# Issuing a second mixture's slots during RWKV, and half of its shared experts behind its blocks, in a macaron network on one core

## The chip, the cores and the metric

The kernel runs on one core of a Trainium2 chip. It is one launch, and what counts is the device time of that launch in microseconds (us). TensorE does matmuls and transposes, VectorE (DVE) and ScalarE (ACT) do elementwise work and read the matmuls' results from PSUM, GpSimd (POOL) issues the indirect DMAs that move rows to and from slots, and SyncE (SP) issues the plain DMAs.

## The reference, cut to what matters

2048 tokens (two sequences of 1024) with 256 features pass through six residual steps, all in float32:

```python
x = L0_attn_x
x = x + 0.5 * L0_ffn(layernorm(x))     # 8 experts, 2 a token, hidden 176, shared hidden 352
x = x + L0_attn(layernorm(x))          # RWKV: time-mix, then channel-mix
x = x + 0.5 * L0_ffn(layernorm(x))     # the same mixture again
x = x + 0.5 * L1_ffn(layernorm(x))     # 32 experts, 6 a token, hidden 96, shared hidden 192
x = x + L1_attn(layernorm(x))          # linear attention
x = x + 0.5 * L1_ffn(layernorm(x))
```

A mixture is a routed part and a shared part, both of the normalized rows:

```python
topk_w, topk_idx = top_k(softmax(x @ gate_w), K)
g = silu(x @ w_gate[e]) * (x @ w_up[e])
routed = sum over chosen e of comb[t, e] * (g @ w_down[e])
shared = silu(x @ sw_gate) * (x @ sw_up) @ sw_down
```

RWKV here has no recurrence over time beyond a shift by one token: `h * mk + shift(h) * (1 - mk)` feeds keys, values and receptances, then the channel-mix does the same with a hidden width of 1024.

## The kernel before

The tokens lie in 16 tiles of 128 rows, `x[0]` to `x[15]`, in SBUF for the whole run. Four tiles (512 tokens) are a *quad*; there are four quads. The tile framework plans the order of the instructions on each engine with a simulated time line: what is written earlier has priority, but an instruction whose inputs are ready in the simulation can be put ahead of one written earlier. Within an engine the planned order is kept on the chip.

**A mixture** (`sparse_moe`) has these parts. `prep(b)` normalizes a quad (L124 to L157), transposes it into `xT` (L163, L420), multiplies it with the router (L424) and chooses the experts (`route`, L181 to L220). `plan(g)` counts rows per expert and gives each (token, expert) pair a slot in an array in DRAM, `xs` (L440 to L528); a quad's plan needs the counts of the quads before it. `scatter(g)` sends the normalized rows to their slots, one indirect DMA for each tile and choice: 8 a quad for L0, 24 for L1 (L538). `owners()` says which expert each block of 128 slots belongs to, once all quads are planned (L562 to L592). `weights(h)` picks the mixing weights (L601 to L608). `shared(t0, t1)` is the shared experts of some tiles (L631, L647, L654, L672; the result is added to `x` at L679). `blocks()` runs the experts' blocks one behind the other, 39 for L0: load the rows (L689), transpose (L698, L702), gate and up (L720), SiLU and product (L621, L622), transpose (L647), down (L737), store to `ys` (L746). `combine(g)` gathers a quad's results as soon as the blocks that can hold its rows are done (L757) and adds them to `x` (L769).

A block's load waits for every slot of its mixture (a dependence added by hand in `fetch`). While blocks are written, `Clock` runs other generators beside them: its own count of time decides between which blocks a quad's gathers or the next mixture's preparation are written, and `issue_after` keeps some of that behind the block just written.

**RWKV** is a list of jobs: time-mix of quad 0, time-mix of 1, channel-mix of 0, time-mix of 2, channel-mix of 1, and so on. `run` writes each job's `main` and, after its second step, the next job's `prep` (norms, transposes and shift). A time-mix's `prep` normalizes `x` into `xl` and that again into `n`. A channel-mix's `prep` also adds `xl` to `x` on GpSimd (L972), and its `main` adds `csr` there (L994), which completes the quad's `x`. All of RWKV's buffers are in one pool that is opened after the first mixture's pool is closed.

The order of the stages is: first L0 mixture (`begin`: prep, plan and scatter of all quads, then owners; shared experts of all 16 tiles; blocks, with gathers beside them), RWKV, second L0 mixture (`begin`, shared experts of all tiles, blocks), then the L1 mixture for two halves of the tokens (A and B), attention, and L1 again. Beside the second L0 blocks, `between` and `first_pass` gather the quads, prepare L1's half A and send its rows (48 indirect DMAs). When the L0 blocks are done, L0's weights are released and L1's down weights take their place.

Of the kernel before, what the change touches and what calls it, by code (L numbers as in the profile page):

```python
# [55 lines left out]
def macaron_kernel(ctx: ExitStack, tc: tile.TileContext, a: dict, out: bass.AP):  # L56
# [23 lines left out]

    numbers_i = const.tile([P, NT], I32, name="numbers_i")
    nc.gpsimd.iota(numbers_i, pattern=[[1, NT]], base=0, channel_multiplier=0)
    numbers = const.tile([P, NT], F32, name="numbers")
    nc.vector.tensor_copy(numbers, numbers_i)
    steps128 = const.tile([P, NT], F32, name="steps128")
    nc.vector.tensor_scalar(steps128, numbers, float(P), None, ALU.mult)

# [16 lines left out]
    nc.vector.tensor_scalar(others128, own128, -1.0, float(P), ALU.mult, ALU.add)  # L104

    row_of_i = const.tile([P, P], I32, name="row_of_i")
    nc.gpsimd.iota(row_of_i, pattern=[[1, P]], base=0, channel_multiplier=0)
    row_of = const.tile([P, P], F32, name="row_of")
    nc.vector.tensor_copy(row_of, row_of_i)
    row128 = const.tile([P, P], F32, name="row128")  # L110
    nc.vector.tensor_scalar(row128, row_of, float(P), None, ALU.mult)

# [267 lines left out]

    def sparse_moe(layer, w, name, x, xs, ys, moe, given=None, out=None):

# [8 lines left out]
        first = [moe_blocks(w, BT * (g + 1)) for g in range(NB)]  # L391
        taken = moe.tile([P, NT, E], F32, tag="taken", name=f"taken_{name}", bufs=2)
        comb = moe.tile([P, NT, E], F32, tag="comb", name=f"comb_{name}", bufs=2)
        slot = moe.tile([P, NT, E], F32, tag="slot", name=f"slot_{name}", bufs=2)
        top = back.tile([P, NT, 8], F32, tag="top", name=f"top_{name}", bufs=2)
        idx = back.tile([P, NT, K], I32, tag="idx", name=f"idx_{name}", bufs=3)
        wk = back.tile([P, NT, K], F32, tag="wk", name=f"wk_{name}", bufs=2)
        who = moe.tile([1, P], I32, tag="who", name=f"who_{name}", bufs=2)
        used = moe.tile([1, 1], I32, tag="used", name=f"used_{name}", bufs=2)
        xn, xT = {}, {}  # L400
        if given is not None:
            xn[0], xT[0] = given
        scattered, stored, groups = [], [], []

        def places(t):

            h, i = divmod(t, HT)
            if h not in xn:
                xn[h] = moe.tile([P, HT, D], F32, tag="xn", name=f"xn_{name}_{h}", bufs=2)
                xT[h] = moe.tile([P, DC, SEQ], F32, tag="xT", name=f"xTs_{name}_{h}", bufs=2)  # L410
            return xn[h], xT[h], i

        def prep(b):
            sub = f"{name}_{b}"
            ts = slice(BT * b, BT * b + BT)
            xb, xbT, o = places(BT * b)
            xb = [xb[:, o + i, :] for i in range(BT)]
            normalize(x[ts], xb, BT, sub)
            for c in range(DC):
                nc.scalar.copy(xbT[:, c, o * P : o * P + TB], transposed(xb, c, sub))  # L420
            lg = bank("pt", f"lg_{sub}")[:, 0 : BT * E].rearrange("p (t e) -> p t e", e=E)
            for i in range(BT):
                for c in range(DC):
                    nc.tensor.matmul(  # L424
                        lg[:, i, :],
                        xbT[:, c, (o + i) * P : (o + i + 1) * P],
                        w["router"][:, c, :],
                        start=(c == 0),
                        stop=(c == DC - 1),
                    )  # L430
            route(w, lg, sub, taken[:, ts, :], comb[:, ts, :])
# [99 lines left out]
        def scatter(g, rank=0):  # L531

            for t in range(BT * g, BT * g + BT):
                xb, _, i = places(t)
                for k in range(K):
                    yield from clock.call(rank)
                    with in_turn():
                        d = nc.gpsimd.indirect_dma_start(  # L538
                            out=xs,
                            out_offset=bass.IndirectOffsetOnAxis(  # L540
                                ap=idx[:, t, k : k + 1], axis=0
                            ),
                            in_=xb[:, i, :],
                            in_offset=None,
                        )
                    clock.called(d)
                    tc.declare_no_dep(
                        d.ins, group=f"slots_{name}", reason="a slot is one pair's"
                    )
                    tc.add_to_no_dep_group(f"slots_{name}", d.ins)  # L550
                    scattered.append(d.ins)
# [135 lines left out]
        def fetch(b):  # L687
            xb = moe.tile([P, D], F32, tag="xb", name=f"xb_{name}_{b}", bufs=XB)
            d = nc.sync.dma_start(out=xb, in_=xs[b * P : (b + 1) * P, :])  # L689
            for s in scattered:  # L690
                tc.add_manual_dep(d.ins, s.name, SYNC, reason="all tokens are at their slots")
            xbs[b] = xb

        def features(b):
            xb = xbs.pop(b)
            px = bank("pb", f"px_{name}_{b}")
            for c in range(DC):
                nc.tensor.transpose(  # L698
                    px[:, c * P : (c + 1) * P], xb[:, c * P : (c + 1) * P], ident
                )  # L700
            xbT = moe.tile([P, DC, P], F32, tag="xbT", name=f"xbT_{name}_{b}", bufs=2)
            nc.scalar.copy(xbT.rearrange("p c t -> p (c t)"), px[:, 0 : DC * P])  # L702
            xbTs[b] = xbT
# [29 lines left out]
        def outward(b):  # L733
            hT, e = bhT.pop(b), ws.pop(b)
            py = bank("py", f"py_{name}_b{b}")[:, 0:D]
            for k in range(C):
# [6 lines left out]
                )  # L743
            yb = moe.tile([P, D], F32, tag="yb", name=f"yb_{name}_{b}", bufs=3)
            clock.did(vector=nc.vector.tensor_copy(yb, py), tensor=mm)
# [58 lines left out]
        def blocks():  # L804
# [21 lines left out]

        return dict(
            prep=prep,
            plan=plan,
# [27 lines left out]
    def shifted(src, g, bias, tag, b, before, name):  # L857


        n = quad(rw["pool"], "xn", f"n_{name}", bufs=1)  # L860
        normalize(src, n, BT, name)
        hT = rw["pool"].tile([P, DC, TB + 1], F32, tag=tag, name=f"hT_{name}", bufs=2)
        if before is None:
# [13 lines left out]
    def mixed(hT, v, tag, name):  # L877

        pool = rw["pool"]
        o = pool.tile([P, DC, TB], F32, tag=tag, name=f"{tag}_{name}", bufs=1)  # L880
        for c in range(DC):
            t = pool.tile([P, TB], F32, tag="mixt", name=f"mixt_{tag}_{name}_{c}", bufs=2)
            nc.scalar.activation(t, hT[:, c, 0:TB], AF.Copy, scale=rw[f"1-{v}"][:, c : c + 1])
# [30 lines left out]
    def time_mix_job(b):  # L914
# [3 lines left out]
        def prep():  # L918
            xl = quad(rw["pool"], "xl", f"xl_{name}", bufs=3)
            normalize(xb, xl, BT, f"{name}_a")  # L920
# [231 lines left out]

    def run(jobs):
        jobs[0][0]()
        for j, (_, main) in enumerate(jobs):
            nxt = jobs[j + 1][0] if j + 1 < len(jobs) else None
            for n, _ in enumerate(main()):
# [3 lines left out]
            if nxt is not None:  # L1161
                nxt()

    xs, ys = {}, {}
# [16 lines left out]

    rwkv = [time_mix_job(0)]
    for b in range(1, NB):
        rwkv += [time_mix_job(b), channel_mix_job(b - 1)]
    rwkv.append(channel_mix_job(NB - 1))
# [38 lines left out]

    with tc.tile_pool(name="rwkvw", bufs=1) as weights:
        with tc.tile_pool(name="moe_L0_0", bufs=1) as pool:
            m = sparse_moe("L0", w0, "L0_0", x, xs["L0"], ys["L0"], pool)
            begin(m)
            load_rwkv(weights)
            for h in range(2):  # L1230
                m["weights"](h)
            every_step(m["shared"](0, NT))
            added = set()
            clock.begin(0, given_rows(m, range(NB), added))
            all_of(m["blocks"]())
            settle(lambda: NB - 1 in added)
        for h in range(2):
# [5 lines left out]
            )  # L1243
        clock.block.clear()
        with tc.tile_pool(name="rwkv", bufs=1) as pool:
            rw["pool"] = pool
            run(rwkv)

# [4 lines left out]

    m0 = sparse_moe("L0", w0, "L0_1", x, xs["L0"], ys["L0"], moe_pool)
    begin(m0)
    for h in range(2):
        m0["weights"](h)
    every_step(m0["shared"](0, NT))

    m1, m2 = {}, {}  # L1260
    added0, summed, ready1, ready2 = set(), {0}, [set(), set()], [set(), set()]
    sent1, sent2 = [set(), set()], [set(), set()]
# [17 lines left out]
    def first_pass(h):  # L1280

        for g in range(2):
            yield from wait(lambda: 2 * h + g in added0)
            if g == 0:
                m1[h] = half(0, h)
            yield from onward(m1[h], g, ready1[h])
# [51 lines left out]
    for h in range(2):  # L1338
        clock.begin(1 + h, first_pass(h))
    all_of(m0["blocks"]())  # L1340
    settle(lambda: 1 in ready1[0])
    l0_stack.close()
# [87 lines left out]
```

## Time and profile before

| what | us |
|---|---|
| median of 3 runs | 1716.1 (1712.1 to 1722.52) |
| profiled execution, whole | 1729.15 |
| its span | 1727.4 |
| TensorE busy (share of the span) | 1334.3 (77%) |
| VectorE busy | 737.4 (43%) |
| ScalarE busy | 625.8 (36%) |
| GpSimd busy | 522.7 (30%) |

The span is the time between the first and the last instruction of the one execution that was profiled. Lines of the profile name a group of instructions by source line, engine, operation and tiles (`out<-in`, buffer numbers left out; `L` in a tile's name stands for L0 or for a numbered use). PEld is TensorE's loading of weights, which overlaps its matmuls. In brackets stands the idle time ahead of an instruction and what ended it; "issue" is a wait for nothing that the profile shows, "remote" a release whose author it cannot name. The granted clock is the share of full speed at which TensorE was allowed to run.

| stretch, us | what runs |
|---|---|
| 0 to 136 | first L0 mixture: routing, slots, shared experts |
| 136 to 241 | its 39 blocks |
| 241 to 257 | last gathers, first time-mix norms |
| 257 to 474 | RWKV |
| 474 to 594 | second L0 mixture: routing, slots, shared experts |
| 594 to 781 | its blocks; L1 half A prepared beside them |
| 781 to 1727 | L1 mixture, attention, L1 mixture |

### The profile page before, as it was taken

How to read it: one execution, taken by the hardware profiler on the slowest of the kernel's cores; microseconds unless marked ns; L12 is line 12 of the kernel's file. 1: busy time of each engine (PE TensorE's matmuls, PEld its weight loads, DVE VectorE, ACT ScalarE, POOL GpSimd, SP SyncE). 2: the span in 40 equal slices, each digit the busy share in tenths (PEclk: the TensorE clock that was granted, in tenths of full speed). 3: DMA queues.
4: the chain of work that ended last, by engine and by line, in shares of the span. 5: the costliest groups of instructions: out<-in, count | busy, mean ns of one | idle time of the engine just before them, and what ended most of it. 6: DMA issues, size and time to landing. Idle time of an engine off the chain costs nothing. (4 is left out here: it accounts for less than half of the span.)

```text
span 1727.4 us, 22283 instructions
## 1 busy us (share of the span) xinstructions
PE 1334.3 (77%) x6100; PEld 1009.8 (58%) x6100; DVE 737.4 (43%) x2510; ACT 625.8 (36%) x1670; POOL 522.7 (30%) x562
## 2 busy tenths in 40 slices
PE   6699967899978998627559768975669994668972
PEld 5577743566666776415449656764357772447951
DVE  4422458555243234215234437432347642425543
ACT  3123346876432333302215334432124442123520
POOL 2400330111133012663350333022744014546055
PEclk8599988899967998767579869886878985888986
DMA  9502439500082033227235545232344332336653
GB/s 297 161 28 86 143 106 330 204 1 0 1 209 70 24 117 99 100 95 207 91 127 181 169 146 156 76 107 78 122 138 147 98 97 87 120 98 207 199 158 97
DMA packets 195164, 214.89 MB, mean 124 GB/s; under 512 B 40892, under 2 KB 178012, under 8 KB 195036
## 3 DMA queue, kind: packets, MB, share of 16 engines
q1 hardware_dynamic: 170460, 146.22, 27.3%
q0 software_dynamic: 24576, 67.14, 12.3%
q8 instruction: 59, 0.97, 0.2%
q14 instruction: 69, 0.57, 0.1%
HBM read 103.04 MB, written 110.23 MB: 123 GB/s over the span
## 5 line engine op out<-in xcount | busy, mean ns | idle before, releaser
L757 POOL DMA_INDIRECT yk_L<-ys_L,idx_L x64 | 61.3, 958 | 288.2 <-DMA ys_L<-yb_L 251.7
L720 PE MATMUL pg_L_b<-L0gu,xbT_L 128*128 x312 | 108.5, 471 | 0.0
L737 PE MATMUL py_L_b<-L0down,hT_L_b 88*128 x312 | 87.4, 405 | 10.0 <-issue 6.4
L631 PE MATMUL pg_L<-L0sgu,xTs_L 128*128 128x352 f32 x256 | 89.2, 488 | 3.7 <-DVE h_L L622 3.7
L538 POOL DMA_INDIRECT xs_L<-xn_L,idx_L x64 | 61.9, 967 | 99.0 <-DVE idx_L L528 42.1
L538 POOL DMA_INDIRECT xs_A<-axl_at,idx_L_1A x48 | 47.2, 982 | 128.1 <-DVE idx_L_1A L528 114.1
L538 POOL DMA_INDIRECT xs_B<-axl_at,idx_L_1B x48 | 46.4, 966 | 129.0 <-DVE idx_L_1B L528 115.0
L757 POOL DMA_INDIRECT yk_L_0A<-ys_A,idx_L_0A x48 | 46.7, 973 | 120.8 <-DMA xb_L_0A<-xs_A 67.5
L737 PEld LDWEIGHTS py_L_b<-L0down,hT_L_b 88*128 88x128 f32 x312 | 62.3, 204 | 33.5 <-issue 9.8
L622 DVE TENSOR_TENSOR h_L_b<-g_L_b,pg_L_b 128x176 f32<-128x176 f32 x78 | 26.1, 336 | 120.1 <-ACT g_L_b L621 85.5
L757 POOL DMA_INDIRECT yk_L_1B<-ys_B,idx_L_1B x48 | 46.0, 958 | 72.6 <-DMA xb_L_1B<-xs_B 50.4
L631 PEld LDWEIGHTS pg_L<-L0sgu,xTs_L 128*128 128x128 f32 x256 | 49.4, 202 | 28.1 <-DVE h_L L622 5.3
L720 PEld LDWEIGHTS pg_L_b<-L0gu,xbT_L 128*128 128x128 f32 x312 | 55.3, 196 | 17.9 <-issue 1.0
L892 PE MATMUL pkk_cm<-mk_cm,w_WkeyT 128*128 128x512 f32 x128 | 62.0, 615 | 2.9 <-ACT sk_cm L984 2.9
L720 PE MATMUL pg_L_0B_b<-L1gu,xbT_L_0B 128*128 x272 | 63.3, 361 | 0.2
L720 PE MATMUL pg_L_1A_b<-L1gu,xbT_L_1A 128*128 x272 | 62.3, 356 | 1.4 <-issue 1.3
L720 PE MATMUL pg_L_0A_b<-L1gu,xbT_L_0A 128*128 x272 | 62.1, 354 | 1.0 <-issue 1.0
L538 POOL DMA_INDIRECT xs_B<-xn_L_0B,idx_L_0B x48 | 46.6, 970 | 52.9 <-DVE ends_L_0B L574 30.3
L737 PE MATMUL py_L_1A_b<-L1down,hT_L_1A_b 96*128 x136 | 48.1, 445 | 17.0 <-issue 13.1
L720 PE MATMUL pg_L_1B_b<-L1gu,xbT_L_1B 128*128 x272 | 60.3, 347 | 0.0
L757 POOL DMA_INDIRECT yk_L_0B<-ys_B,idx_L_0B x48 | 46.4, 966 | 45.6 <-DVE x L769 29.4
L757 POOL DMA_INDIRECT yk_L_1A<-ys_A,idx_L_1A x48 | 46.9, 977 | 43.3 <-DVE x L769 26.9
(641 smaller groups left out, 3381.5 us busy)
## 6 DMA issues: line engine op xcount, KB each, us to landing
xs_A<-zero SPq DMA_DIRECT2D x1, 10112.0 KB
xs_B<-zero SPq DMA_DIRECT2D x1, 10112.0 KB
xb_L<-xs_L SPq DMA_DIRECT2D x78, 128.0 KB
ys_L<-yb_L SPq DMA_DIRECT2D x78, 128.0 KB
xb_L_0A<-xs_A SPq DMA_DIRECT2D x68, 128.0 KB
ys_A<-yb_L_0A SPq DMA_DIRECT2D x68, 128.0 KB
xb_L_0B<-xs_B SPq DMA_DIRECT2D x68, 128.0 KB
ys_B<-yb_L_0B SPq DMA_DIRECT2D x68, 128.0 KB
```

Of the source, the lines that this page charges most:

```text
L538: d = nc.gpsimd.indirect_dma_start(out=xs, out_offset=bass.IndirectOffsetOnAxis(ap=idx[:, t, k : k + 1], axis=0), in_=xb[:, i, :], in_offs ...
L622: nc.vector.tensor_tensor(dst, g, pg[:, width : 2 * width], ALU.mult)
L631: nc.tensor.matmul(pg, xbT[:, c, i * P : (i + 1) * P], w["sgu"][:, c, u, :, :].rearrange("p z w -> p (z w)"), start=(c == 0), stop=(c == D ...
L720: nc.tensor.matmul(pg, xbT[:, c, :], w["gu"][:, c, bass.ds(e, 1), :, :].rearrange("p e z h -> p (e z h)"), start=(c == 0), stop=(c == DC - 1),
L737: mm = nc.tensor.matmul(py, hT[0:HP, k, :], w["down"][:, bass.ds(e, 1), k, :].rearrange("p e d -> p (e d)"), start=(k == 0), stop=(k == C ...
L757: d = nc.gpsimd.indirect_dma_start(out=yk, out_offset=None, in_=ys[0 : n * P, :], in_offset=bass.IndirectOffsetOnAxis(ap=idx[:, t, k : k + ...
L892: nc.tensor.matmul(ps, w[:, c, oc * P : (oc + 1) * P], src[:, c, :], start=(c == 0), stop=(c == DC - 1),)
```

## The change

The second L0 mixture is made before RWKV is run, and the slots of quads 0, 1 and 2 are issued behind the channel-mix of that quad (`slots_of`, run from `behind`). Their normalized rows are in RWKV's one-buffer `xn` tile and their transposed rows in a one-buffer `xTe`; since neither outlives the quad, `again(b)` repeats norm and transposes for the shared experts later. Quad 3 is prepared behind RWKV as before, then come the owners.

Of both L0 mixtures' shared experts, tiles 0 to 7 are done ahead of the blocks and tiles 8 to 15 behind them. In the second mixture, `again(2)` comes behind the blocks too, and the preparation of L1's half B waits for `summed0`.

The first two time-mix `prep`s are run by the clock beside the first L0 blocks, each once its quad's results are added (`first_jobs`). The buffers that they use (`xn`, `xl`, `h1T`, `mk`, `mixt`) lie in a new pool, `rwkv_in`, that is opened ahead of the first mixture's pool. To make room, index tiles at the start are merged and some of the mixture's small tiles have one buffer.

```diff
-    def sparse_moe(layer, w, name, x, xs, ys, moe, given=None, out=None):
+    def sparse_moe(layer, w, name, x, xs, ys, moe, given=None, out=None, bufs=2, early=None):
...
+        def features_of(b, xb, xbT, o, sub):
+            normalize(x[BT * b : BT * b + BT], xb, BT, sub)
+            for c in range(DC):
+                nc.scalar.copy(xbT[:, c, o * P : o * P + TB], transposed(xb, c, sub))
+        def again(b):
+            xb, xbT, o = places(BT * b)
+            features_of(b, [xb[:, o + i, :] for i in range(BT)], xbT, o, f"{name}_{b}_again")
         def prep(b):
             sub = f"{name}_{b}"
             ts = slice(BT * b, BT * b + BT)
-            xb, xbT, o = places(BT * b)
-            xb = [xb[:, o + i, :] for i in range(BT)]
-            normalize(x[ts], xb, BT, sub)
-            for c in range(DC):
-                nc.scalar.copy(xbT[:, c, o * P : o * P + TB], transposed(xb, c, sub))
+            if early is not None and b < NB - 1:
+                xb, o = early(sub), 0
+                xbT = rw["pool"].tile([P, DC, TB], F32, tag="xTe", name=f"xTe_{sub}", bufs=1)
+            else:
+                xb, xbT, o = places(BT * b)
+                xb = [xb[:, o + i, :] for i in range(BT)]
+            sent[b] = xb
+            features_of(b, xb, xbT, o, sub)
...
     def shifted(src, g, bias, tag, b, before, name):
-        n = quad(rw["pool"], "xn", f"n_{name}", bufs=1)
+        n = quad(rw["in"], "xn", f"n_{name}", bufs=1)
...
-    def run(jobs):
-        jobs[0][0]()
+    def run(jobs, begun, behind):
         for j, (_, main) in enumerate(jobs):
-            nxt = jobs[j + 1][0] if j + 1 < len(jobs) else None
+            nxt = jobs[j + 1][0] if j + 1 < len(jobs) and j + 1 >= begun else None
             for n, _ in enumerate(main()):
                 if nxt is not None and n == 1:
                     nxt()
                     nxt = None
             if nxt is not None:
                 nxt()
+            if j in behind:
+                behind[j]()
...
+    def slots_of(b):
+        def slots():
+            m0["prep"](b)
+            m0["plan"](b)
+            every_step(m0["scatter"](b))
+        return slots
     for b in range(1, NB):
+        behind[len(rwkv) + 1] = slots_of(b - 1)
         rwkv += [time_mix_job(b), channel_mix_job(b - 1)]
...
-            every_step(m["shared"](0, NT))
+            every_step(m["shared"](0, HT))
             added = set()
+            def first_jobs():
+                for b in range(begun):
+                    yield from wait(lambda: b in added)
+                    rwkv[b][0]()
             clock.begin(0, given_rows(m, range(NB), added))
+            clock.begin(1, first_jobs())
             all_of(m["blocks"]())
+            all_of(m["shared"](HT, NT))
             settle(lambda: NB - 1 in added)
...
+        m0 = sparse_moe("L0", w0, "L0_1", x, xs["L0"], ys["L0"], early_pool, bufs=1,
+            early=lambda sub: quad(rw["in"], "xn", f"xn_{sub}", bufs=1))
+        run(rwkv, begun, behind)
...
-    m0 = sparse_moe("L0", w0, "L0_1", x, xs["L0"], ys["L0"], moe_pool)
-    begin(m0)
+    m0["home"]["pool"] = moe_pool
+    slots_of(NB - 1)()
+    m0["owners"]()
+    for b in range(2):
+        m0["again"](b)
+    every_step(m0["shared"](0, HT))
     for h in range(2):
         m0["weights"](h)
-    every_step(m0["shared"](0, NT))
...
     def first_pass(h):
         for g in range(2):
             yield from wait(lambda: 2 * h + g in added0)
             if g == 0:
+                yield from wait(lambda: h in summed0)
                 m1[h] = half(0, h)
...
     all_of(m0["blocks"]())
+    m0["again"](2)
+    all_of(m0["shared"](HT, NT))
+    summed0.add(1)
     settle(lambda: 1 in ready1[0])
     l0_stack.close()
```

## The prediction

> **What bounds the kernel now.** I read the page first, then the busy times of stretches cut at the stage borders, then TensorE's timeline around each border, then the waits inside the one stretch that looked wrong. The stage borders come from TensorE's own tiles: the first L0 mixture's blocks (`pg_L_b`) run from 136.3 to 240.8 us, RWKV's first projection (`pk_tm`) starts at 257.2, its last matmul ends at 473.4, the second L0 mixture's blocks start at 594.2, and the first L1 blocks (`pg_L_0A_b`) at 815.1.
>
> Busy times of stretches (columns: stretch, its length, then busy us and instructions of PE, PEld, DVE, ACT, POOL, then the granted TensorE clock, the DMA share and GB/s):
>
> ```profile
> 136.00:241.00 105.00, 100.37 (x473) 74.86 (x471) 40.57 (x114) 38.52 (x118) 22.93 (x24) 1.00 0.38 119
> 241.00:257.00 16.00, 1.94 (x8) 1.57 (x8) 11.78 (x48) 8.12 (x14) 7.66 (x8) 0.56 0.27 82
> 257.00:308.00 51.00, 40.11 (x97) 20.75 (x98) 42.37 (x79) 33.71 (x47) 5.23 (x8) 0.80 0.94 334
> 308.00:474.00 166.00, 160.61 (x568) 104.60 (x566) 76.89 (x175) 110.56 (x153) 19.16 (x26) 0.98 0.11 40
> 474.00:538.00 64.00, 48.20 (x252) 40.13 (x253) 26.31 (x177) 17.62 (x35) 23.87 (x25) 0.64 0.65 162
> 538.00:594.00 56.00, 56.00 (x237) 41.19 (x236) 16.35 (x53) 17.39 (x57) 7.72 (x8) 0.95 0.10 33
> 688.00:781.00 93.00, 45.88 (x193) 30.97 (x192) 25.29 (x103) 17.40 (x41) 53.91 (x56) 0.70 0.28 97
> ```
>
> TensorE is the bound in blocks, in the later part of RWKV (160.6 busy of 166) and in the shared experts. It is not the bound in three places, and there the change works: the 16 us after the first blocks (2 busy), the 64 us of the second mixture's routing (48 busy, at a granted clock of 0.64, so much less in work), and the 93 us from 688 on, where GpSimd is busiest.
>
> TensorE's timeline (start, us, engine, line, operation):
>
> ```profile
> 112.99 3.12 PE L631 MATMUL pg_L<-L0sgu,xTs_L 128*128 128x352 f32 x10
> 120.98 3.12 PE L631 MATMUL pg_L<-L0sgu,xTs_L 128*128 128x352 f32 x10
> ...
> 257.22 6.77 PE L892 MATMUL pk_tm<-mk_tm,w_WkT 128*128 128x512 f32 x8 [3.44 <-DVE mk_tm L884]
> 272.19 3.70 PE L892 MATMUL pk_tm<-mk_tm,w_WkT 128*128 128x512 f32 x8 [0.45 <-DVE mk_tm L884]
> ...
> 475.39 1.06 PE L163 MATMUL pt_L<-ident,xn_L 128*128 128x128 f32 x8 [1.99 <-DVE xn_L L154]
> 594.23 1.35 PE L720 MATMUL pg_L_b<-L0gu,xbT_L 128*128 x4
> ```
>
> The same place in the pattern of shared experts comes back after 8.0 us, which is two tiles: 4.0 us a tile. From the last RWKV matmul to the second blocks are 594.2 - 473.4 = 120.8 us. GpSimd's first slot of that mixture goes out only at 495.6:
>
> ```profile
> 495.56 1.02 POOL L538 DMA_INDIRECT xs_L<-xn_L,idx_L  x1 [20.77 <-ACT xTs_L L420]
> ```
>
> And in 688 to 781 the waits are not for data that take long to make:
>
> ```profile
> DVE h_L_b L622 <- remote: 23.7, 2, 19.6
> PE pg_L_0A L631 <- issue: 21.7, 1, 21.7
> ACT g_L_b L621 <- remote: 22.3, 1, 22.3
> ```
>
> While GpSimd sends trains of 24 slots (688 to 719, 738 to 768), what TensorE finished reaches ScalarE and VectorE 5 to 22 us late, and the mixture's last blocks crawl: block 33 starts at 716.4 where the even pace of 2.49 us would put it at 676.
>
> **The change, part by part** (times of the profiled execution: span 1727.4, whole 1729.15 us; the median of the runs shown is 1716.1, 0.8% lower, so a difference is carried over to it as it stands).
>
> *First mixture.* Eight tiles of shared experts leave the front: 8 x 4.0 = 32 us, and the blocks start at 104 in place of 136.3. Nothing else holds them there: the last slot goes out at 89.1 and the load of the first block's rows is issued at 91.6. The 32 us come back behind the blocks, where TensorE had the 16 us with 2 busy. So the time-mix could begin at 257.2 - 16 = 241, if the first two quads' norms cost nothing beside the blocks. They do cost: a norm of the L1 kind beside blocks held block 26 back by 13.3 - 2.5 = 11 us (656.2 to 669.5), a quad's gathering and adding by 1.8 us (196.3 after 192.3). Two quads: 4 to 22 us, taken at 8 because there is no routing in them. Net -8. The first eight projections also find a warm clock (6.77 against 3.70 us, -3) and the mix for the keys is made early (-1). Sum -12; bounds -25 (all hidden, and the vector work of 257 to 308 shortened too) and 0.
>
> *Slots in RWKV.* Norm, eight transposes, 16 router matmuls, counts and ranks, and eight slots for each of three quads now lie in a stretch where TensorE has 5 us of slack in 166. TensorE's own share is 5.6 us for the first quad at a warm clock (1.06 + 2.17 + 0.34 + 1.62 + 0.36) and about 6.2 for a later one (estimate: its rows at half clock, halved): 18 us for three. Above that lie the in-order hand-overs. Alone, one quad followed another every 14 us (counts at 501.9, 515.6, 529.6), 42 for three; an L1 quad's norm and plan beside blocks took 11 + 6.6 us, 52 for three. I take 28, nearer the low end: RWKV offers the planner other matmuls between the hand-overs, the blocks' pipeline did not. GpSimd's slots (8 x 1.27 = 10 us a quad) lie in a queue that is 19 of 166 us busy; behind a slot that waits for its indices stand the residual adds (L972, L994), and `csr`, which has two buffers, waits for those. The norms of time-mix and channel-mix now share one `xn` buffer with rows that the slots' DMAs still read. Both are hidden as long as the planner puts the next channel-mix's norm, whose inputs are ready a whole job earlier, ahead of the slots.
>
> ScalarE pays here too: each quad needs the square root and the exponential between SiLU and sigmoid, some four table loads. The row: a load took 1.28 us (at 478.85), and the activation behind it started 0.01 us after it ended, so 5 us a quad beside 110.6 busy of 166; that is inside the 28. The Trainium skill ("ScalarE: Activation LUTs", What ACT_TABLE_LOAD costs) adds a drain of about 1.38 us to each switch; by it three quads would cost an estimated 17 us more and the sum below would nearly vanish. The trace shows no such drain, so I leave it out.
>
> The skill speaks against the slots in another way ("SBUF — State Buffer", SBUF: two separate sides): GpSimd cannot write descriptors while VectorE runs certain copies, and an indirect DMA beside them may take about 3100 ns where 620 was normal. Here, with VectorE 41% busy (474 to 538), slots kept their 962 ns (median of 64, longest 1140), and RWKV's VectorE is 46% busy; no charge. By the page, 24 slots would hold `xn` an estimated 60 us longer in all.
>
> *Before the second blocks.* 120.8 us become what one quad needs: idx 21 us after RWKV's end as now (495.6), owners till about 27 (535.7 to 538.5 now, some 5 us behind the last count), and behind that what remains of eight shared tiles when four tiles' first products are done by then, as they were at 492: 4 x 2.4 + 8 x 1.6 = 23 us. That is 50; the last quad's slots end at 32 and are covered. The repeated norms and transposes of quads 0 and 1 (16 transposes, 2 us) hide in the 27 us. So -71 (bounds -78 and -60).
>
> *Behind the second blocks.* Quad 2's repeated transposes (3 us with copies) and eight shared tiles, 32 us: +35. TensorE had 47 us idle in 688 to 781, but that idle time is the late signals; its queue is in order, and the shared experts stand behind the blocks that wait. When the last train ended at 768, blocks and L1's own shared tiles were still to do, so I charge all 35; the other end is 0. Quad 2's added rows (L769) now also wait for its repeated norm, and group B's first norm for the shared half; group B's slots ended at 900 and its blocks began at 1002, so 35 us are covered.
>
> Removed index tiles at the start: five small instructions of 0.13 to 0.54 us ahead of data that arrive at 2.9 us; nothing. The zero fills (23 MB) start earlier and end long before the first slot in RWKV; nothing.
>
> Sum: -12 + 28 - 71 + 35 = **-20 us**: 1709 profiled, **1696** for the median.
>
> **The rivals.** *The tail is hidden:* the shared half runs in the 47 idle us. For it: that much is idle. Against: the order of the queue. Then -20 - 35 = -55: 1661.
>
> *Nothing left:* the slots cost as an L1 quad beside blocks, 17.4 us each, 52: -12 + 52 - 71 + 35 = +4, no change that can be measured.
>
> *Slower: the single `xn` buffer.* If buffers are handed out in the written order, the channel-mix norm waits until a quad's slots have left: 21 us chain + 10 us of slots, 31 a quad with nothing covering it, 93 for three: -12 + 93 - 71 + 35 = +45: 1761. With the time-mix of some 20 us between as cover it is less. It decides from (12 + 71 - 35) / 3 = 16 us a quad. For it: TensorE is full there and VectorE's and ScalarE's queues are in order. Against: the trace has the second quad's time-mix statistics (247.6) ahead of the first quad's mixes (256.4), so work moves ahead of its written place.
>
> **How the numbers follow.** 0.5% (8.6 us) is about what a measurement of this kernel can tell from no change. My forecast (9 to 45 us gained, 1671 to 1707) gets 0.47, the hidden tail 0.12, nothing left 0.15, slower 0.26. Faster is 0.59, same 0.15, slower 0.26. The terms' best ends give -25 + 18 - 78 + 0 = -85, their worst 0 + 52 - 60 + 35 = +27, and the buffer rival +45. Leaving out about a tenth on each side, I give 1645 to 1750.
>
> **What would show it.** Right: first blocks at about 104; `pk_tm` around 249; the last RWKV matmul at 473.4 - 12 + 28 = about 489; the second blocks 50 us after it, about 540; `pg_L_0A_b` about 20 us earlier than 815.1, with the L0 shared tiles between the last L0 block and L1's shared tiles. Wrong: idle stretches of TensorE over 10 us in RWKV ended by `xn` or by an indirect DMA (the buffer rival); L0's shared half finished before the second train ends (hidden tail); or late signals spreading into RWKV once slots go out there.

## The result, and the profile after

The changed kernel takes 1767.03 us (median of 4 runs, 1763.81 to 1769.4) where the kernel before takes 1717.87 us (4 runs): a ratio of 1.0287, 95% interval 1.0249 to 1.0324. The forecast was 1696; it went the other way, to where the rival of the single `xn` buffer (1761) had put it. The profiled execution has a span of 1766.4 us, 39 us over the one before. The medians differ by 49: the profiled execution before, of 1729.15 us, is longer than each of the 4 runs (1722.52 at most). What follows explains the 39.

The stage borders, from TensorE's tiles (us; the start of the matmul named):

| border | before | after | after - before | foreseen |
|---|---|---|---|---|
| first L0 blocks | 136.3 | 103.8 | -32.5 | 104 |
| first projection (`pk_tm`) | 257.2 | 255.5 | -1.7 | 249 |
| channel-mixes of quads 0 to 3 (`pkk_cm`) | 307.6, 357.6, 404.9, 441.9 | 302.5, 389.5, 478.2, 503.2 | -5, +32, +73, +61 | |
| last RWKV matmul | 473.0 | 548.5 | +75.5 | 489 |
| second L0 blocks | 594.2 | 612.3 | +18.1 | 540 |
| last of these | 736.1 | 759.3 | +23.2 | |
| first L1 blocks (`pg_L_0A_b`) | 815.1 | 885.2 | +70.1 | 795 |
| last of these | 984.9 | 1022.6 | +37.7 | |
| end | 1727.4 | 1766.4 | +39 | |

Busy times of stretches of the changed kernel, in the columns used before (stretch, its length, then PE, PEld, DVE, ACT, POOL, the granted TensorE clock, the DMA share, GB/s):

```profile
302.00:342.00 40.00, 39.51 (x140) 26.53 (x141) 16.87 (x41) 26.38 (x37) 5.45 (x8) 0.95 0.57 190
342.00:390.00 48.00, 30.80 (x95) 19.17 (x94) 27.15 (x89) 16.78 (x28) 11.76 (x13) 0.66 0.06 23
390.00:415.00 25.00, 25.00 (x82) 15.46 (x81) 4.24 (x8) 14.24 (x21) 0.10 (x1) 0.98 0.00 1
415.00:478.00 63.00, 39.91 (x138) 26.07 (x136) 30.87 (x104) 23.43 (x35) 14.08 (x16) 0.72 0.05 17
550.00:613.00 63.00, 49.88 (x227) 37.31 (x228) 23.85 (x112) 21.07 (x54) 10.77 (x12) 0.76 0.61 150
759.00:885.00 126.00, 79.23 (x347) 56.51 (x346) 45.80 (x178) 30.94 (x73) 53.25 (x55) 0.75 0.40 118
885.00:1022.00 137.00, 111.08 (x615) 97.09 (x615) 50.97 (x169) 52.03 (x202) 34.74 (x36) 0.84 0.49 151
```

RWKV, which had TensorE busy for 160.6 of 166 us, now has two holes: 342 to 390, where quad 0's slots are, and 415 to 478, where quad 1's are. In them TensorE is 64% and 63% busy, at a granted clock of 0.66 and 0.72; in the full stretch between them the clock is 0.98. No other engine is full in the holes either: behind TensorE, VectorE is the busiest, at 57% and 49%.

TensorE's timeline in the first hole (start, us, engine, line, operation, and in brackets the idle time ahead and what ended it):

```profile
342.09 3.60 PE L908 MATMUL pv_tm<-mv_tm,w_WvT 128*128 128x512 f32 x8
352.18 0.66 PE L156 MATMUL pt_L<-ident,xn_L 128*128 128x128 f32 x2 [6.49 <-DVE xn_L L147]
353.87 1.54 PE L156 MATMUL pt_L<-ident,xn_L 128*128 128x128 f32 x6 [1.02 <-ACT xn_L L143]
356.55 3.63 PE L436 MATMUL lg_L<-L0router,xTe_L 128*128 128x8 f32 x16 [1.14 <-ACT xTe_L L415]
363.17 0.34 PE L452 MATMUL count_L<-ones,taken_L 128*8 128x1 f32 x8 [2.99 <-DVE taken_L L202]
...
365.17 3.76 PE L908 MATMUL pr_tm<-mr_tm,w_WrT 128*128 128x512 f32 x4
...
376.63 4.67 PE L920 MATMUL po_tm<-w_WoT,rv_tm 128*128 128x256 f32 x12 [1.66 <-DVE rv_tm L968]
384.00 1.78 PE L156 MATMUL pt_cm<-ident,n_cm 128*128 128x128 f32 x8 [2.70 <-DVE n_cm L147]
```

The routing steps of quad 0 (`pt_L`, `lg_L`, `count_L`) stand ahead of the third time-mix's receptances (`pr_tm`) in TensorE's queue. Each step waits for VectorE or ScalarE, and what is ready behind it waits too: `mr_tm`, from which the receptances are made, is written by 332.2. And four `pr_tm` products then take 3.76 us; in RWKV's full stretches four such products take 1.88. Only at 384.0 come the transposes of the channel-mix's norm (`pt_cm`), and with them the 25 us of solid work that the hole had lacked. Their norm itself was held up, as all engines' timeline shows:

```profile
353.02 0.30 ACT L132 ACTIVATE rstd_cm<-mv_cm,eps 128x4 f32<-128x4 f32 x1
...
371.31 1.01 POOL L549 DMA_INDIRECT xs_L<-xn_L,idx_L  x1 [27.73 <-DVE idx_L L540]
...
380.72 0.96 POOL L549 DMA_INDIRECT xs_L<-xn_L,idx_L  x1 [0.31 <-issue]
...
383.22 1.09 ACT L143 ACTIVATE n_cm<-xl_tm,shift_cm,rstd_cm 128x256 f32<-128x256 f32 x2 [9.00 <-DMA xs_L<-xn_L,idx_L]
```

The channel-mix's statistics are there at 353.3. Its norm `n_cm` is written 30 us later, into the buffer from which quad 0's eight slots have just been read. The 9.00 us in the bracket are only what ScalarE had been idle; the wait of the data is the 30. In the second hole the statistics are there at 435.0, quad 1's slots leave from 460.4 to 470.2, and the norm starts at 471.7. There the wait stands alone in TensorE's timeline:

```profile
457.70 3.74 PE L920 MATMUL po_tm<-w_WoT,rv_tm 128*128 128x256 f32 x14 [0.23 <-DVE slot_L L529]
472.49 1.97 PE L156 MATMUL pt_cm<-ident,n_cm 128*128 128x128 f32 x8 [11.04 <-DVE n_cm L147]
```

Quad 2's slots open no hole. `behind` runs them after the last but one channel-mix, and the last one's norm is written ahead of them. From the channel-mix of quad 2 to RWKV's end are 70.3 us, and 68.0 in experiment 3, which has no slots in RWKV; the two spacings before that are 87.0 and 88.7 against 46.9 and 49.1.

### The profile page after: what moved, and what is told of

The parts are those of the page before. It is cut to its first block, busy times and chain, and to the rows that moved or that the text cites. A ratio compares the mean times of both kernels' runs of the same rounds, so it can differ in the third digit from the quotient of the medians.

```text
span 1766.4 us, 22400 instructions
## 1 busy us (share of the span) xinstructions
PE 1352.0 (77%) x6124; PEld 1016.8 (58%) x6124; DVE 743.3 (42%) x2543; ACT 625.5 (35%) x1683; POOL 523.3 (30%) x561
## 5 line engine op out<-in xcount | busy, mean ns | idle before, releaser
L731 PE MATMUL pg_L_b<-L0gu,xbT_L 128*128 x312 | 112.2, 484 | 0.2
L748 PEld LDWEIGHTS py_L_b<-L0down,hT_L_b 88*128 88x128 f32 x312 | 64.2, 211 | 32.0 <-issue 11.6
L665 ACT COPY hT_L_b<-ph_L_b 88x256 f32<-88x256 f32 x78 | 28.6, 368 | 88.9 <-PE ph_L_b L658 47.8
```

The source lines that it names most:

```text
L665: nc.scalar.copy(hT[0:m, lo:hi, :].rearrange("p k t -> p (k t)"), pt[0:m, lo * P : hi * P])
L731: nc.tensor.matmul(pg, xbT[:, c, :], w["gu"][:, c, bass.ds(e, 1), :, :].rearrange("p e z h -> p (e z h)"), start=(c == 0), stop=(c == DC - 1),
L748: mm = nc.tensor.matmul(py, hT[0:HP, k, :], w["down"][:, bass.ds(e, 1), k, :].rearrange("p e d -> p (e d)"), start=(k == 0), stop=(k == C ...
```

## The experiments

The runs were made on several chips: on that of experiments 1 to 4 the kernel before takes 1488, on the others 1717 to 1741. So times are compared as ratios to the kernel before on the same chip, and stages by their length; RWKV, from the start of its first projection to that of its last matmul, runs at one pace on all of them (211.8, 210.7, 210.7 and 210.9 us in the versions without slots: 3, 7, 10 and 12). It took 215.8 us before (215.0 in experiment 6) and 293.0 in the change (293.1 in 4 and 5).

**1. Slots' rows in a buffer of their own.**

```diff
-                e2 = pool.tile([P, TB], F32, tag="e2", name=f"e2_{name}_{oc}", bufs=1)
+                e2 = dp
...
-                av = pool.tile([P, TB], F32, tag="av", name=f"av_{name}_{oc}", bufs=1)
+                av = rv[:, oc, :]
...
-            early=lambda sub: quad(rw["in"], "xn", f"xn_{sub}", bufs=1),
+            early=lambda sub: quad(rw["in"], "xe", f"xe_{sub}", bufs=1),
```

> The early slots' rows get a buffer of their own; to make room, two scratch tiles of the time-mix are written in place of others. In the changed kernel the channel-mixes of quads 0, 1 and 2 start 87.0 and 88.7 us apart (50.0 and 47.3 before), and RWKV ends at 549. Buffer theory: the channel-mix norm waits until eight slots have been read out of xn, so with its own buffer the norm goes at about 354 in place of 383, the spacing falls to 60 to 65 us, RWKV ends at 495 to 505, and the time is 1710 to 1725. Hand-over theory (the router's chain in TensorE's in-order queue holds the time-mix's rest): spacing stays over 80 and the time within 1755 to 1770.

Measured: ratio 1.0145 (1.0103 to 1.0188), channel-mixes 77.3 and 67.9 us apart, RWKV 265.4 us. That lies between the two theories: the buffer is worth 28 us of RWKV, not 50. VectorE's and TensorE's timelines of this version say where the rest went (the norm, then its transposes):

```profile
354.51 0.64 DVE L147 TENSOR_SCALAR n_cm<-xl_tm,rstd_cm,shift_cm 128x256 f32<-128x256 f32 x2
```

```profile
347.87 1.94 PE L156 MATMUL pt_L<-ident,xe_L 128*128 128x128 f32 x8 [7.03 <-DVE xe_L L147]
352.65 3.64 PE L436 MATMUL lg_L<-L0router,xTe_L 128*128 128x8 f32 x16 [2.84 <-ACT xTe_L L415]
362.10 0.34 PE L452 MATMUL count_L<-ones,taken_L 128*8 128x1 f32 x8 [5.82 <-DVE taken_L L202]
...
368.74 1.11 PE L156 MATMUL pt_cm<-ident,n_cm 128*128 128x128 f32 x4
```

The norm is now done at 355.2, as the buffer theory said. But its transposes start at 368.7: they stand behind the routing steps in TensorE's queue, and TensorE waits 5.8 us for `taken_L` with them ready.

**2. Slots one job later** (those of quads 0 and 1; those of quad 2 stay where they are).

```diff
-        behind[len(rwkv) + 1] = slots_of(b - 1)
+        behind[min(len(rwkv) + 2, 2 * NB - 2)] = slots_of(b - 1)
```

> The slots of quads 0 and 1 are issued one job later, behind the next channel-mix's norm; the one xn buffer stays. Buffer theory: the channel-mix no longer waits for slots, the next time-mix's norm does, and that has a whole channel-mix of 25 us as cover: spacing of the channel-mixes 55 to 65 us, RWKV ends at 490 to 510, time 1710 to 1730. Hand-over theory: the same chain stands in the same queues one job later, spacing over 80, RWKV's end about 549, time 1755 to 1770.

Measured: ratio 0.9982 (0.9961 to 1.0003); channel-mixes 45.6 and 60.7 us apart, RWKV 239.0 us. The first spacing is under the pace before (50.0). Without slots RWKV takes 211 us, so slots cost 82 in the change and 28 here: with the one shared buffer, place alone is worth 54. TensorE's timeline after it shows the cover:

```profile
344.82 3.60 PE L908 MATMUL pkk_cm<-mk_cm,w_WkeyT 128*128 128x512 f32 x8
...
352.12 1.04 PE L156 MATMUL pt_L<-ident,xn_L 128*128 128x128 f32 x8
353.93 1.98 PE L908 MATMUL pkk_cm<-mk_cm,w_WkeyT 128*128 128x512 f32 x4 [0.77 <-ACT sk_cm L1000]
...
360.65 1.40 PE L436 MATMUL lg_L<-L0router,xTe_L 128*128 128x8 f32 x12
361.91 1.11 PE L920 MATMUL po_tm<-w_WoT,rv_tm 128*128 128x256 f32 x4
```

The same steps lie between products of the channel-mix, whose norm is now written ahead of them. From 345 to 390 no gap reaches 2 us, and the eight transposes take 1.04 us in place of 2.2.

**3. No slots in RWKV** (the line with `behind[...]` is taken out, the second mixture begins behind RWKV as before, so no norm is repeated; the first mixture's part of the change and both halved shared experts stay).

> All four quads' slots of the second mixture are issued behind RWKV, as before the change; the first norms beside the blocks and the halved shared experts stay. If the slots alone lengthen RWKV, it ends at 465 to 472 (473.4 before, 549 changed) and the second blocks start 85 to 92 us behind it, at about 555 to 562 (612 changed), so the time is 1712 to 1722. If the norms moved beside the blocks or the clock lengthen RWKV too, it ends above 490 and the time is over 1730.

Measured: ratio 0.9933 (0.9909 to 0.9958); RWKV 250.6 to 462.4, second blocks 87.1 us behind it. The slots alone lengthen RWKV: 293 - 211 = 82 us, and they take 87.1 - 63 = 24 off the stretch behind it. Without them the change is 0.7% faster than the kernel before. Busy times of RWKV in the change, in this version and in version 2:

```profile
255.50:548.90 293.40, 239.82 (x825) 153.57 (x823) 132.92 (x370) 141.93 (x207) 44.37 (x55) 0.85 0.26 86
250.60:462.80 212.20, 197.92 (x681) 125.34 (x679) 117.73 (x251) 142.54 (x199) 23.83 (x34) 0.97 0.32 106
252.20:491.60 239.40, 217.10 (x825) 139.80 (x823) 133.44 (x370) 156.25 (x219) 44.02 (x55) 0.96 0.31 106
```

Three quads' slots are 144 matmuls (825 - 681). In version 2 they make TensorE 19 us busier and leave it idle for 8 us more. In the change the same matmuls make it 42 us busier, at a clock of 0.85 and not 0.96, and idle for 39 us more.

**4. All of the second mixture's shared experts in front of its blocks** (slots in RWKV as in the change).

```diff
+    m0["again"](2)
-    every_step(m0["shared"](0, HT))
+    every_step(m0["shared"](0, NT))
...
-    summed0 = {0}
+    summed0 = {0, 1}
...
-    m0["again"](2)
-    all_of(m0["shared"](HT, NT))
-    summed0.add(1)
```

> The second mixture's shared experts all run ahead of its blocks, the slots in RWKV stay. Second blocks at about 646 to 650 (612 changed). Tail theory (behind the blocks the half costs its 32 us and more, 47 by the borders): the first L1 blocks start 10 to 15 us earlier than 885 and the time is about 1750 to 1758. Train theory (the first L1 blocks gained 33 us because the second pair's slots had mostly gone by the time that they ran, so any earlier start is given back): time 1764 to 1772.

Measured: ratio 1.0369 (1.0346 to 1.0392); RWKV 293.1 us; second blocks 95.0 us behind it, 32 more than in the versions with half in front. From the last L0 block to the first L1 block are 48.3 us, where versions 1 to 3 on the same chip take 89.2, 82.4 and 79.0; the first L1 blocks then last 111.7 us and not 97 to 98. So both theories hold a part: the tail costs 31 to 41 us there, and 14 come back inside the first L1 blocks. The change itself was not run on this chip, so the two ratios can't be set against each other. For the changed kernel itself the same three lengths are 63.8 (121.2 before), 126 (79) and 137 (170).

**5 and 6. The change and the kernel before, once more**, for their borders beside the versions.

> The changed kernel itself, beside the versions of it, for their common scale. Its RWKV is that of the version with all shared experts in front (ends at 542.5 there), its second blocks should then start at 604 to 608 and the time be 1527 to 1540 where the kernel before takes 1488 (ratio 1.025 to 1.035). If the shared half behind the blocks costs more than it saved in front, the ratio is over 1.037.

> The kernel before, for its stage borders on the same scale as the versions: 1488. If the first norms beside the blocks and the half behind them are worth nothing, the first projection starts at 248 to 252 and RWKV ends at 460 to 466, as in the version without slots (250.6, 462.4); if they are worth the 12 I gave them, 260 to 264 and 472 to 476.

Measured: the change again 1.0277 (1.0238 to 1.0315), with RWKV of 293.1 us, second blocks at 616.0 and the first L1 blocks at 894.8. The kernel before has its first projection at 258.4 and its last RWKV matmul at 473.4, in the version without slots on the same chip (7) 255.0 and 465.7: the first mixture's part is worth 8 us at RWKV's end (5 to 6 by version 10). The stages beside the mixtures' slots are not so steady: from the last L0 to the first L1 block the kernel before takes 69.0 us here and 79.0 in its first profile, and the change 132.9 and 126.

**7. No slots, with half of the shared experts written between the routing steps of quads 2 and 3.**

> The version without slots in RWKV, with the first half of the shared experts written between the third and fourth quad's routing steps instead of behind all of it. Idle theory: TensorE's gaps and half clock in the 87.1 us between RWKV and the second blocks (73.4 busy at a clock of 0.71) are what is lost, and the shared tiles fill them: 68 to 76 us, time 1460 to 1468. Queue theory: each routing step then waits behind a shared tile, the chain is stretched by what is filled in: 84 to 92 us, time 1475 to 1482.

Measured: 91.9 us between RWKV and the second blocks, ratio 0.9884 (0.9836 to 0.9931). The queue theory's 84 to 92: filling did not shorten the stretch, which takes 86.3 us without it (12). In 12 the planner already has four tiles' first products ahead of the first quad's counts. Why those that were written between the later quads gained nothing, no run separates.

**8. Slots one job later, and the last quad's routing between the shared tiles of quads 0 and 1.**

```diff
...
-    slots_of(NB - 1)()
-    m0["owners"]()
...
     for b in range(2):
         m0["again"](b)
-    every_step(m0["shared"](0, HT))
+    front = m0["shared"](0, HT)
+    m0["prep"](NB - 1)
+    steps(front, 3)
+    m0["plan"](NB - 1)
+    every_step(m0["scatter"](NB - 1))
+    steps(front, 1)
+    m0["owners"]()
+    every_step(front)
```

`steps(front, n)` takes the next n steps of the shared experts, one for each tile; the later place of the slots is written as in 2.

> The version with the slots one job later, and the last quad's routing written between the shared tiles of quads 0 and 1, whose repeated norms come first. Idle theory: the 63.1 us between RWKV and the second blocks fall to 48 to 54, time 1473 to 1479. Queue theory: 60 to 66 us, time 1485 to 1490.

Measured: ratio 0.9893 (0.9856 to 0.993); 51.9 us between RWKV and the second blocks, where 2 has 63.1. Here the fill works. In the change the first shared product follows owners and repeated norms, in this version it precedes the last quad's routing. TensorE's timelines of the two around RWKV's end, the change first:

```profile
557.68 1.94 PE L156 MATMUL pt_L<-ident,xn_L 128*128 128x128 f32 x8 [8.79 <-DVE xn_L L147]
...
577.30 4.90 PE L642 MATMUL pg_L<-L0sgu,xTs_L 128*128 128x352 f32 x8
```

```profile
499.96 1.94 PE L156 MATMUL pt_L_again<-ident,xn_L 128*128 128x128 f32 x8 [4.10 <-DVE xn_L L147]
...
503.27 4.09 PE L642 MATMUL pg_L<-L0sgu,xTs_L 128*128 128x352 f32 x8
...
510.00 1.04 PE L156 MATMUL pt_L<-ident,xn_L 128*128 128x128 f32 x8
```

RWKV's last matmul starts at 548.5 and 495.5: the first shared product comes 29 us behind it in the change, 8 us here.

**9. All three: own buffer, one job later, filled** (the edits of 1, 2 and 8).

> Slots one job later, their rows in a buffer of their own, the last quad's routing written between shared tiles. With slots one job later RWKV took 239 to 241 us from its first projection, 211 without slots. Buffer theory: part of the 28 to 30 left is the next time-mix's norm waiting for xn (third channel-mix 60.7 us behind the second, where 49 is the pace without slots): RWKV 228 to 234, ratio to before 0.982 to 0.986. Work theory: what is left is TensorE's own 19 us of routing products and the hand-overs, no buffer: RWKV 238 to 242, ratio 0.987 to 0.992.

Measured: 1693.06 us where the kernel before takes 1721.64, ratio 0.9845 (0.9814 to 0.9876); RWKV 234.2 us, 52.6 from there to the second blocks. It is 1.5% faster than the kernel before. With the slots in the better place the buffer is worth 5 to 7 us of RWKV (239.0 in 2 and 241.2 in 8, which share it). Busy times of its RWKV and of the stretch behind it:

```profile
255.00:490.00 235.00, 214.60 (x825) 140.22 (x823) 135.42 (x390) 160.55 (x223) 44.39 (x55) 0.96 0.32 108
490.00:542.00 52.00, 46.09 (x231) 33.42 (x231) 20.44 (x93) 21.61 (x53) 11.41 (x13) 0.93 0.73 177
```

**10. Only the first mixture's part** (as 3, and all 16 shared tiles of the second mixture in front of its blocks).

> Only the first mixture's part of the change: half of its shared experts behind its blocks, the first two time-mix norms beside them; routing and all shared experts of the second mixture ahead of its blocks as before. By the borders of the versions without slots RWKV ends 8 us earlier than before (465.7 and 473.4), so the ratio is 0.993 to 0.997. If the halved shared experts of the second mixture are worth what they moved out of the front, this is slower than the version without slots (0.9933); if they are an even trade (32 out of the front, 43 in between the blocks of L0 and L1, 32 back inside the first L1 blocks), the two are within 0.3% of each other.

Measured: ratio 0.9986 (0.9965 to 1.0008), no change that can be measured, and a little above the expected 0.993 to 0.997, though RWKV ended at 467.7. Against 12, where the second half lies behind the blocks: 119.7 us before the second blocks and 86.3 with the half moved; 69.1 and 116.8 from the last L0 to the first L1 block; first L1 blocks of 168.2 and 137.4. Moving the half thus takes 33, adds 48 and gives back 31: about 16 gained, 0.9% of the time. The ratios of 3 (0.9933) and 10 differ by half a per cent, but 3 ran on the faster chip.

**11. Slots one job later, without GpSimd's part in RWKV** (norms, routing and plans as in 2; the 24 indirect DMAs leave behind RWKV).

> Slots one job later, but only norms, routing and plans lie in RWKV; GpSimd's 24 slots of quads 0 to 2 go out behind RWKV from the repeated norms. Only RWKV's length is read from it: GpSimd theory (the slots stand ahead of the residual adds and hold csr and xn): 218 to 228 us. TensorE theory: 236 to 241, as with the slots.

Measured: RWKV 237.0 us. GpSimd's slots, and what they hold up, are 2 to 4 of the 28 us that remain in the better place. By the rows in 3, most of the rest is TensorE's own time for the products, 19 us.

**12. Control for the buffer: no slots, scratch tiles in place.**

> A control for the versions with a buffer of their own for the slots' rows: no slots in RWKV, but the two scratch tiles of the time-mix written in place as there. Only RWKV's length is read (211 us without slots and with separate tiles). If writing in place costs nothing: 210 to 213. If it holds the time-mix's chain on VectorE and ScalarE: 216 or more, and the buffer's share in the versions is then larger by that much than their difference.

Measured: RWKV 210.9 us. Writing in place costs nothing, so 1 and 9 show the buffer alone.

## Why the prediction was wrong, step by step

The terms, against the profiled executions of the pair (borders) and the experiments:

| step | predicted | measured | from |
|---|---|---|---|
| first mixture, to RWKV's end | -12 | -8 | 6 and 7 |
| slots in RWKV | +28 | +82 | 293 - 211 |
| stretch before the second blocks | -71 | -57 | 121.2 to 63.8 |
| second blocks | 0 | +5 | 141.9 to 147.0 |
| half behind the blocks | +35 | +47 | 79 to 126 |
| first L1 blocks | 0 | -32 | 169.8 to 137.4 |
| later stages | 0 | +2 | remainder |
| sum | -20 | +39 | |

The second term is steady from run to run (293.0 and 293.1, 210.7 to 211.8). The terms behind the second blocks are good to some 10 us, as 5 and 6 show.

**The step that failed is the second: "I take 28, nearer the low end: RWKV offers the planner other matmuls between the hand-overs".** The planner finds them only where the slots are issued one job later: there they cost 28 us (experiment 2). Where the change puts them they cost 82. TensorE's own share, put at 18, was right: version 2 shows 19. What failed is the rest: 10 us were left for the hand-overs, and the wait for the `xn` buffer was put at nothing; together they cost 64 in the change. That version 2 comes to the very 28 is luck, as it is not the order that was predicted for.

What the runs put in its place is two waits, told apart by the two buffers and the two places:

| RWKV, us (211 without slots) | shared `xn` | own buffer |
|---|---|---|
| slots as in the change | 293 | 265 (1) |
| slots one job later | 239 (2), 241 (8) | 234 (9) |

With the buffer shared, the channel-mix's norm waits for slots that are at the end of the longest chain in the stage; freeing it is worth 28 us where the change has the slots, and 5 to 7 in the better place. With the buffer free, place is still worth 31: the norm is done, but its transposes stand behind routing steps in TensorE's queue, which wait for VectorE. That it is TensorE's queue is read from the timeline of 1; the orders of VectorE and ScalarE moved with it, and no run changes one queue alone.

**The slower rival had the price, and half of the mechanism.** Its 93 us for three quads stand against 82, and 1761 against 1767. In part that is luck: not three quads cost 31 us each, but quads 0 and 1 some 40 each and quad 2 about 2, and the buffer alone is 28 of the 82. Its condition was that buffers are handed out in the written order; the 30 us between `rstd_cm` and `n_cm`, ended by the slots' DMAs, show that. What I held against it, the second quad's statistics running ahead of the first quad's mixes, was the wrong evidence: statistics need no buffer of the stage before and no place in TensorE's queue. The same holds here: `st_cm` ran ahead too, and `n_cm` could not. And "hidden as long as the planner puts the next channel-mix's norm ... ahead of the slots" named the condition without asking what the planner does with a buffer for which the slots were written first.

**The first mixture.** The blocks start at 103.8, as predicted. But a quad's norm beside the blocks put 11.6 us between blocks 25 and 26 and 10.3 between 33 and 34, together 17 beyond the pace of 2.49, where 8 was taken. In all, the first block's start and the last one's are 121.9 us apart and not 97.2: 25 more, over the upper bound of 22. (The lower bound rests on 1.8 us for a quad's gathering; the row named for it, 196.3 after 192.3, gives 1.5.) `pk_tm` so came at 255.5 and not at 249. Some of it returned as a shorter RWKV, 211 and not 215 to 216 us, as the version without slots shows.

**Before the second blocks.** 63.8 in place of 50. The routing went as predicted: the owners are done 27.5 us behind RWKV's end, against 27 (the 21 us to the first slot were 22 by its own row, 495.6 after 473.4). The step "four tiles' first products are done by then" failed: in the kernel before four quads' routing left room for them, in the change one quad's routing, owners and the repeated norms come first, and the first shared product is at 577.3. Written ahead, as in 8 and 9, the stretch takes 52 us; so the size was right for an order that the change does not have.

**Behind the second blocks.** The half costs 47 and not 35, and 32 come back, which was not in the sum: the first L1 blocks used to start at 815.1 and ran beside both trains of group B's slots (809 to 839, 870 to 900), and now start at 885.2 beside one. The other runs on the slower chips agree, though none moves the trains alone: 168 us where both fall into these blocks (6 and 10), 134 to 137 where one does (5, 7, 8, 9, 11 and 12). Predicted with the stretch before the blocks, -36; measured, with the 5 us of the second blocks, -37. Here two errors cancelled, and the sum was right by luck.

**The signs.** Of the signs named for an error, "idle stretches of TensorE over 10 us in RWKV ended by `xn` or by an indirect DMA" came: the one of 11.0 us in the second hole, ahead of `pt_cm`, for an `n_cm` that waited for the slots' DMAs. Late signals did not spread into RWKV: in the waits there is no remote release between 256 and 550. The slots' own time stayed as argued, with a median of 960 ns in the change, so the charge by the Trainium skill's page "SBUF — State Buffer" (SBUF: two separate sides) was rightly left out. So was the drain that its page "ScalarE: Activation LUTs" (What ACT_TABLE_LOAD costs) adds to each switch: the activation after a load starts 0.01 us behind it where its data are there. The four more loads a quad did not come either: RWKV had 46 before, 41 in the change and 53 in version 2, which is the faster.

## What to carry to other kernels

Work moved beside a busy stage costs little more than its engine time (28 us for 19 here, against 82) only if something ready stands between its hand-overs in the in-order queues; so look up what stands right behind each of its steps, and issue it behind the stage's next long run of products, not ahead of it. A buffer that is shared with a DMA's source is free only when the DMA has left, which is the end of the chain that computes its addresses: price the wait of the next user from that end, not from the buffer's last write. That some instruction runs ahead of its written place is evidence only for instructions that need the same buffers and queues.

## What was not expected of the hardware

The time of one and the same kernel differs by 13 to 15% between chips: 1488 for the kernel before on one, 1717 to 1741 on the others. The difference lies in the stages beside GpSimd's long trains of indirect DMAs: without slots in RWKV, the second L0 blocks, the stretch behind them and the first L1 blocks take 122, 79 and 97 us on the one chip (3) and 150, 117 and 137 on another (12). It is not in RWKV, nor to speak of in the first L0 blocks (102.4 to 221.3 and 102.0 to 224.3, borders in us). On the slower chips the waits of these kernels hold 193 to 266 us of releases that the profile calls remote; on the faster one the waits have none. Waits between the second L0 blocks and the first L1 blocks, of version 8 on a slower chip (engine, tile, line, us in total, times, longest):

```profile
ACT g_L L632 <- remote: 22.0, 3, 12.3
ACT hT_L_0A L665 <- remote: 21.2, 1, 21.2
DVE x L690 <- remote: 16.6, 1, 16.6
DVE h_L L633 <- remote: 13.3, 1, 13.3
```

Version 2 on the faster chip has none of these lines, takes 82 us for the stretch where version 8 takes 125, and its GpSimd issues the slots at the same pace of 1.27 us. What makes the releases late on one chip and not on another, no run here shows.

A hole in TensorE's work costs twice: in the stretch from 342 to 390 the granted clock was 0.66, and a product with 512 columns took 0.94 us (3.76 for four) where it takes 0.47 in version 2. By the rows in 3 that second part is 23 us of the change's RWKV: 239.8 us busy and 217.1 for the same 825 matmuls.
